# Four fused image layers on one core: layer 0's output statistics by ACT, attention stored compactly, a third exponential tile, and another order in search and q

## The chip, the cores and the metric

The kernel runs on one core of a Trainium2 chip. A core has a matrix engine (TensorE, PE in the tables), a vector engine (VectorE, DVE), a scalar engine for activations (ScalarE, ACT), a general engine (GpSimd, POOL) and an engine that here only issues transfers (SyncE, SP). Each engine executes its own instructions in its own order and waits on semaphores for the others. DMA queues move data between the device's memory and the on-chip memory SBUF; products of PE land in PSUM, which has eight banks of 512 fp32 columns on 128 partitions, and ACT and DVE read them there. The metric is device time in microseconds (us) of one execution; of several executions the median is given.

## The reference

The input is 16 images of 64 x 64 tokens with 256 channels, in fp32. Four layers follow each other, each added to its input, and each working on a group-normalized copy of it (32 groups of 8 channels; mean and variance over the group's channels and all tokens of an image):

```
def _gn(v, G=32, eps=1e-5):                      # (v - mean) / sqrt(var + eps), by image and group

# layer 0: the nearest of 1024 codes, by distance
indices = argmin(sum(x*x) + sum(e*e) - 2 x @ e);   quantized = e.T[indices]
# layer 1: attention within each image row of 64 tokens
attn = sigmoid(einsum('bhik,bhjk->bhij', f, g));   out = einsum('bhij,bhjo->bhio', attn, h)
# layer 2: a gate from a softmax over all 4096 tokens
sim = x0[:, :, None] * x1[:, None, :];   sm = softmax(sim, axis=1)
gate = sigmoid(einsum('bn,bnm->bm', x2, sm));   out = gate * x
# layer 3: linear attention with 4 heads of 32
q = softmax(q, over a head's 32) * SCALE;   k = softmax(k, over tokens)
context = einsum('bhdn,bhen->bhde', k, v);   out = einsum('bhde,bhdn->bhen', context, q)
out = layernorm(out @ w_out + b_out) * gamma + beta
```

f, g and h are projections of the tokens to 32, 32 and 256 channels; x0, x1 and x2 are projections to one number per token; q, k and v to 128 each.

## The kernel before

**Stages.** An image goes through six stages, written as Python generators: `stats0` (statistics of the input), `stage1` (layer 0, called search below), `layer1`, `rows2` and `stage2` (layer 2's rows and exponentials), `gate2` (layer 2's gate, applied), `stage3` (layer 3). Between stages the image lies in device memory, as eight chunks of 512 tokens, transposed: a chunk is a tile of 128 partitions x 2 halves of the channels x 512 tokens. Each stage also gathers the statistics that the next stage's normalization needs.

**What sets the order.** Each generator yields after a piece of work with a number, the piece's share of the stage. A planner at the end of `tile_net_kernel` gives every stage of every image a start and a length in units of one image's search (`task`, with LAG1, LEN1 and the like), and a heap then takes the piece that is due next. So six stages of different images are interleaved. That order is a priority: the tile framework's scheduler sets each engine's order of instructions by it and by what is ready, and `tc.high_priority` lifts a block above the rest. Loads are issued on SP, stores of some results on ACT's queue, gathers on POOL's.

**Buffers.** A pool has rings of buffers, by tag; a tile waits until the ring's oldest is free. PSUM has four single banks (`bank`) for nearly every product and two double ones (`wide`).

**Search** (`stage1`, one image: 8 chunks of 4 token tiles of 128). For each token tile PE computes pd, the products with 1024 codes, in a double bank (L382); ACT writes nn, minus the norms of codes and token (L377); DVE adds both and takes the maximum (L389, a custom instruction), then its index (L394); POOL gathers the code's row onto the tokens (L395). Between the tiles stand a chunk's other steps: `load` of the transposed chunk, `tokens` (load of the tokens), `norm` (ACT normalizes and squares, L327 and L330; PE sums the squares, px, L336; ACT copies them, xrow, L341; PE transposes, pxt, L343), `norm_rows` (DVE copies the norms, L348) and `back`: PE transposes the chunk with its codes back to channels (pt, L357), ACT copies it from PSUM (L360), DVE takes `bn_stats` of it (`chunk_stats`, L254), and ACT's queue stores it (L363). `back(ch - 1)` is called after the third tile of chunk ch, `norm(ch + 1)` after the second. `gn_finish` makes scale, minus mean and their product for the next layer of these statistics, by small products with group matrices.

**Layer 1.** `attend` computes f and g (pfg, L465) and h (ph, L476) of a chunk, and scores of two image rows at a time (psc, L494): 128 x 128 products, of which only the two diagonal blocks of 64 x 64 are used. ACT takes the Tanh of those blocks into one of two attention tiles `attn`, whose other blocks stay zero (L497), and scales them (L500). `mix` multiplies h by the whole 128 x 128 tile (po, L509), and DVE adds the result to the chunk (L513).

**Layer 2's exponentials.** For 32 token tiles and two halves of the tokens, ACT writes the exponentials of 2048 products into a tile ex (L619, with a sum), and DVE multiplies them by x2 and sums (L622). ex has two buffers.

**Layer 3.** For each chunk: k's products and exponentials, q and v (pqv, L751), then the exponentials of q over a head, its sum and normalization (L770 to L776, DVE, POOL and ACT), a product with k's exponentials (pc, L780). `queries(ch - 1)` transposes the normalized q and stores it. After the last chunk come `queries(7)`, and, at high priority, the context product with the output weights and a small Gram matrix. The second loop (`form`, `variance` and the output products po, L849) reads q again.

`put_row` makes a row of 256 values in three bf16 parts, `h_row`, `qv_row` and `x_row`, kept twice side by side; a product with ones adds it to two token tiles.

Of the kernel before, what the change touches and what calls it, by code (L numbers as in the profile page):

```python
# [9 lines left out]
F32 = mybir.dt.float32  # L10
BF16 = mybir.dt.bfloat16
# [5 lines left out]
P = 128  # L17
C = 256
# [23 lines left out]
def kernel(  # L42
# [82 lines left out]
    def row_tile(name):  # L125
        t = const.tile([P, 2, C], BF16, name=name)
        nc.gpsimd.memset(t, 0.0)
        return t

    h_row, qv_row, x_row = row_tile("h_row"), row_tile("qv_row"), row_tile("x_row")  # L130

    def put_row(dst, v, weight, tag, plus=None):
# [11 lines left out]
        nc.scalar.copy(dst[0:PARTS, :, :], row.unsqueeze(1).to_broadcast([PARTS, 2, C]))  # L144
# [43 lines left out]
    w_src = w_qkv.rearrange("(k p) (s n) -> p k s n", p=P, s=3)  # L188


    gam = s3p.tile([P, C], F32, tag="v2", name="gam", bufs=5)
    nc.scalar.dma_start(out=gam, in_=gamma.rearrange("(o n) -> o n", o=1).to_broadcast([P, C]))

    def centred(src, name):
        t = const.tile([P, 2, C], F32, name=name)
        nc.scalar.dma_start(out=t[:, 0, :], in_=src)
        m = small.tile([P, 1], F32, tag="cen", name=f"cen_{name}")
        nc.vector.tensor_reduce(m, t[:, 0, :], AX.X, ALU.add)
        nc.vector.tensor_scalar(m, m, -1.0 / C, None, ALU.mult)
        nc.vector.tensor_scalar(t[:, 0, :], t[:, 0, :], m, None, ALU.add)  # L200
        nc.vector.tensor_tensor(t[:, 1, :], t[:, 0, :], gam, ALU.mult)
        return t

    wo2 = centred(w_out, "wo2")


    bo2 = centred(b_out.rearrange("(o n) -> o n", o=1).to_broadcast([P, C]), "bo2")
    nc.vector.tensor_scalar(bo2, bo2, float(DH ** 0.5 / HEADS), None, ALU.mult)
# [27 lines left out]
    attn = []  # L236
    for n in range(2):
        t = const.tile([P, CH, P], F32, name=f"attn_{n}")
        nc.vector.memset(t, 0.0)
        attn.append(t)  # L240

# [14 lines left out]
    def gn_finish(st, kind, b):  # L256

        tag = f"{kind}_{b}"
        mv = small.tile([P, NK, 2], F32, tag="gn_mv", name=f"mv_{tag}")
        for k in range(NK):  # L260
            nc.vector.bn_aggr(mv[:, k, :], st[:, k, :, :].rearrange("p c s -> p (c s)"))
        mean = mv[:, :, 0]
# [45 lines left out]
    def stage1(b):  # L308
        tag = f"s1_{b}"
        scale, _, nbias = norm0.pop(b)  # L310
# [39 lines left out]
        st1 = stats_tile(1, f"st1_{tag}")  # L350
        x1_d[b] = []

        def back(ch):
            for k in range(NK):
# [5 lines left out]
                nc.scalar.copy(xt[ch][:, k, :], pt)  # L360
            chunk_stats(st1, xt[ch], ch)
# [10 lines left out]
        for ch in range(NCHUNK):  # L372
            for t in range(CH):
# [27 lines left out]
                if t == 1:  # L401
                    if ch + 1 < NCHUNK:
                        norm(ch + 1)
                        yield 2
# [535 lines left out]
```

## Time and profile before

| what | us |
|---|---|
| three runs | 6006.36, 5981.41, 6005.67; median 6005.67 |
| the profiled execution | 5985.76 |
| its span, first to last instruction | 5984.0 |
| largest groups: exponentials with sum on DVE (L622) / on ACT (L619) | 2369.4 / 2138.8 |
| pd on PE (L382) | 2013.5 |
| maximum and index on DVE (L389, L394) | 620.5 and 623.5 |
| nn on ACT (L377) | 585.1 |
| POOL's gathers (L395) | 1084.0 |
| mean granted TensorE clock | 0.949 of full speed |

A row of the profile gives a line, the engine, the operation, the tiles written and read, how often, the busy time and mean duration, and then the idle time of the engine just before such instructions with what ended it. An fp32 product shows as two records on PE, so 2048 products of pd are 4096 records; their ends are modelled, and successive ones overlap. PEld is PE's loading of weights. The reading of an accumulator is an instruction of its own on ACT and DVE.

### The profile page before, as it was taken

How to read it: one execution, taken by the hardware profiler on the slowest of the kernel's cores; microseconds unless marked ns; L12 is line 12 of the kernel's file. 1: busy time of each engine (PE TensorE's matmuls, PEld its weight loads, DVE VectorE, ACT ScalarE, POOL GpSimd, SP SyncE). 2: the span in 40 equal slices, each digit the busy share in tenths (PEclk: the TensorE clock that was granted, in tenths of full speed). 3: DMA queues.
4: the chain of work that ended last, by engine and by line, in shares of the span. 5: the costliest groups of instructions: out<-in, count | busy, mean ns of one | idle time of the engine just before them, and what ended most of it. 6: DMA issues, size and time to landing. Idle time of an engine off the chain costs nothing.

```text
span 5984.0 us, 73947 instructions
## 1 busy us (share of the span) xinstructions
PE 5310.6 (89%) x25167; PEld 3208.0 (54%) x25167; DVE 5132.9 (86%) x7270; ACT 4756.8 (79%) x7138; POOL 1873.7 (31%) x1314
## 2 busy tenths in 40 slices
PE   8978798989989899998989989898999989887777
PEld 3535355545556465554646556464655646464445
DVE  6589698899989899898989989898998989888862
ACT  4578597878888797888979788797988879787763
POOL 3222224233332333323333332433333333312231
PEclk9989899999999999999999999999999999998788
DMA  6453645665656657565665746566475655545543
GB/s 185 143 160 112 209 132 186 187 187 158 207 165 201 194 160 227 149 210 163 197 212 156 224 151 207 172 199 203 153 223 160 204 183 172 188 140 176 170 144 111
DMA packets 521359, 1059.10 MB, mean 177 GB/s; under 512 B 52504, under 2 KB 266392, under 8 KB 512792
## 3 DMA queue, kind: packets, MB, share of 16 engines
q1 hardware_dynamic: 406288, 885.11, 44.6%
q0 software_dynamic: 73728, 67.14, 7.8%
q10 hardware_dynamic: 40968, 102.13, 4.5%
q8 instruction: 200, 3.28, 0.2%
q14 instruction: 175, 1.43, 0.1%
HBM read 751.18 MB, written 303.04 MB: 176 GB/s over the span
## 4 chain that ended last, share of the span: by engine, by line
PE 48%; DVE 21%; ACT 15%; issue 7%; DMA 5%; POOL 4%; ACTq 0%; SPq 0%; POOLq 0%; DVEq 0%
PE pd_s L382 16%; DVE ex_s L622 10%; ACT ex_s L619 6%; PE ph_l L476 4%; PE pqv_s L751 4%; PE po_s L849 3%; DVE i_s L394 2%; PE pk_s L729 2%; PE pr_r L567 2%; DVE nd_s L389 2%; PE po_l L509 2%; POOL xc_s L395 2%; PE pvr_s L829 1%; DVE st_s L254 1%; PE pc_s L780 1%
## 5 line engine op out<-in xcount | busy, mean ns | idle before, releaser
L622 DVE CUSTOM_DVE_ANT_0 ex_s<-ex_s,x2b 128x2048 f32<-128x2048 f32 x1024 | 2369.4, 2318 | 135.9 <-ACT ex_s L619 133.5
L619 ACT ACTIVATE ex_s<-x0b,nmax_s,x_r 128x2048 f32<-128x2048 f32 x1024 | 2138.8, 2089 | 64.7 <-DVE num_s L622 55.0
L382 PE MATMUL pd_s<-e,xn_s 128*128 128x512 f32 x4096 | 2013.5, 621 | 87.6 <-DVE m L389 63.8
L395 POOL DMA_INDIRECT xc_s<-in_emb_rows,i_s x512 | 1084.0, 2117 | 1962.9 <-DVE i_s L394 1460.6
L382 PEld LDWEIGHTS pd_s<-e,xn_s 128*128 128x128 f32 x4096 | 750.6, 196 | 830.4 <-issue 655.0
L389 DVE CUSTOM_DVE_ANT_0 nd_s<-pd_s,nn_s 128x1024 f32<-128x1024 f32 x512 | 620.5, 1212 | 114.8 <-PE pd_s L382 85.4
L394 DVE FIND_INDEX8 i_s<-m,nd_s 128x8 uint32<-128x1024 f32 x512 | 623.5, 1218 | 0.0
L377 ACT ACTIVATE nn_s<-ne,nx_s 128x1024 f32<-128x1024 f32 x512 | 585.1, 1145 | 10.6 <-DVE nx_s L348 3.4
L476 PE MATMUL ph_l<-wh_l,xt_l 128*128 128x256 f32 x2048 | 534.6, 396 | 28.6 <-DVE xt_l L513 20.6
L751 PE MATMUL pqv_s<-wqv_s,xk_s 128*128 128x256 f32 x2048 | 491.9, 381 | 2.9 <-ACT xt_s L360 2.9
L476 PEld LDWEIGHTS ph_l<-wh_l,xt_l 128*128 128x128 f32 x2048 | 381.7, 194 | 155.1 <-issue 61.2
L751 PEld LDWEIGHTS pqv_s<-wqv_s,xk_s 128*128 128x128 f32 x2048 | 388.4, 191 | 130.1 <-issue 63.3
L832 POOL TENSOR_TENSOR lrs_s<-lrs_s,mhalf 128x4 f32<-128x4 f32 x128 | 187.6, 1465 | 651.5 <-ACT lrs_s L831 638.0
L849 PE MATMUL po_s<-wctx_s,qo_s 128*128 128x256 f32 x1024 | 329.4, 412 | 63.5 <-ACT y_s L852 59.8
L852 ACT ACTIVATE y_s<-po_s,lrs_s 128x256 f32<-128x256 f32 x512 | 236.0, 470 | 147.5 <-PE po_s L849 104.3
L327 ACT ACTIVATE xn_s<-xt_s,nb_n,s_n 128x512 f32<-128x512 f32 x256 | 202.4, 806 | 108.2 <-DMA xt_s<-in_xT 98.6
L776 POOL TENSOR_TENSOR qv_s<-qv_s,qd_s 128x512 f32<-128x512 f32 x128 | 167.2, 1307 | 385.3 <-DVE qd_s L775 312.8
L509 PE MATMUL po_l<-attn,h_l 128*128 128x128 f32 x2048 | 280.7, 283 | 7.3 <-DVE m L389 5.2
L509 PEld LDWEIGHTS po_l<-attn,h_l 128*128 128x128 f32 x2048 | 259.9, 195 | 45.8 <-issue 22.1
L849 PEld LDWEIGHTS po_s<-wctx_s,qo_s 128*128 128x128 f32 x1024 | 178.0, 199 | 194.5 <-ACT y_s L852 123.9
L729 PE MATMUL pk_s<-xk_s,wk_s 128*128 128x512 f32 x512 | 256.6, 623 | 0.0
L860 DVE TENSOR_TENSOR y_s<-pxo_s,y_s 128x512 f32<-128x512 f32 x256 | 174.1, 683 | 91.4 <-ACT y_s L852 91.3
(197 smaller groups left out, 7707.6 us busy)
## 6 DMA issues: line engine op xcount, KB each, us to landing
xs_s<-in_xT SPq DMA_DIRECT2D x128, 512.0 KB
xt_s<-in_xT SPq DMA_DIRECT2D x128, 512.0 KB
xc_s<-in_x SPq DMA_DIRECT2D x128, 512.0 KB
x_s<-xt_s ACTq DMA_DIRECT2D x128, 512.0 KB
xt_l<-x_s SPq DMA_DIRECT2D x128, 512.0 KB
x_l<-xt_l SPq DMA_DIRECT2D x128, 512.0 KB
xr_r<-x_l SPq DMA_DIRECT2D x128, 512.0 KB
xg_g<-x_l SPq DMA_DIRECT2D x128, 512.0 KB
```

The source lines that it names most:

```text
L377: nc.scalar.activation(nn, ne2, AF.Identity, bias=nx2[ch][:, t : t + 1])
L382: nc.tensor.matmul(pd[:, cols], lhsT=xn[ch][:, k, t * P : (t + 1) * P], rhs=e2[:, k, cols], start=(k == 0), stop=(k == NK - 1),)
L389: nc.vector.tensor_tensor_reduce(out=nd, in0=pd, in1=nn, scale=1.0, scalar=-3.0e38, op0=ALU.add, op1=ALU.max, accum_out=m8[:, 0:1],)
L394: nc.vector.max_index(i8, m8, nd)
L395: nc.gpsimd.indirect_dma_start(out=xc[ch][:, t, :], out_offset=None, in_=emb_rows, in_offset=bass.IndirectOffsetOnAxis(ap=i8[:, 0:1], axis=0),
L476: nc.tensor.matmul(ph[:, t, :], lhsT=X[:, k, t * P : (t + 1) * P], rhs=wh_n[:, k, :], start=(t % 2 == 0 and k == 0), stop=False, skip_grou ...
L509: nc.tensor.matmul(po[:, k, t * P : (t + 1) * P], lhsT=hs[ch][:, t, k * P : (k + 1) * P], rhs=at[:, t, :], start=True, stop=True,)
L619: nc.scalar.activation(ex, x0b, AF.Exp, bias=nmax[:, T : T + 1], scale=x01[:, T, 1:2], accum_out=den[:, h, T : T + 1])
L622: nc.vector.tensor_tensor_reduce(out=ex, in0=ex, in1=x2b, scale=1.0, scalar=0.0, op0=ALU.mult, op1=ALU.add, accum_out=num[:, h, T : T + 1],)
L729: nc.tensor.matmul(pk, lhsT=wk_n[:, k, :], rhs=xt[:, k, :], start=(k == 0), stop=(k == NK - 1))
L751: nc.tensor.matmul(pqv[:, j, :], lhsT=xt[:, k, t * P : (t + 1) * P], rhs=wqv_n[:, k, :], start=(j == 0 and k == 0), stop=False, skip_group ...
L849: nc.tensor.matmul(po[:, j, :], lhsT=qT[:, t * P : (t + 1) * P], rhs=wctx[:, 1, :], start=True, stop=True)
```

## The change

- **Statistics of layer 0's output.** In `back`, ACT's copy from PSUM also gives the sum over the tokens, and a second activation squares the same bank in place, shifted by layer 0's mean, and gives the sum of squares. `chunk_stats` is no longer called there. At the end of `stage1` five small DVE operations make mean and variance from the sums, and `gn_ends`, the second half of `gn_finish`, goes on from them.
- **Compact attention.** The attention tile holds only the 64 x 64 blocks: two image rows on the two halves of the partitions. Scores are products of 64 x 64; ACT's Tanh and scaling work on 128 partitions at once; `mix` makes two products with 64 rows each where there was one with 128, into two banks, and DVE's addition reads them in the chunk's order. The two zeroed `attn` tiles are gone.
- **Room.** The rows `h_row`, `qv_row`, `x_row` are kept once and read twice (`twice`); w_out and b_out are kept without their copy scaled by gamma, which is multiplied in once per image; two small tiles share buffers with others (wT with wk_n, gram with ctx_bd); the ring v2 has four buffers instead of five. ex has three buffers instead of two.
- **Order in search.** `back(ch - 1)` is called after the second tile of a chunk, `norm(ch + 1)` after the third, `norm_rows` after the fourth.
- **Order in q.** The sum, reciprocal and multiplication that normalize q become `normalize`, called for a chunk when the next one begins; `queries` of the last chunk is called after the high-priority block.
- **Planner.** Layer 1 of image 0 gets a length of 0.2 instead of 0.35. In `stage2` the gate's yields are split in two.

```diff
         def back(ch):
...
-                nc.scalar.copy(xt[ch][:, k, :], pt)
-            chunk_stats(st1, xt[ch], ch)
+                nc.scalar.activation(xt[ch][:, k, :], pt, AF.Copy, accum_out=st1[:, 0, k, ch : ch + 1])
+                nc.scalar.activation(
+                    pt, pt, AF.Square, bias=nshift[:, k : k + 1], accum_out=st1[:, 1, k, ch : ch + 1]
+                )
...
-                if t == 1:
-                    if ch + 1 < NCHUNK:
-                        norm(ch + 1)
-                        yield 2
-                if t == 2:
+                if t == 1 and ch > 0:
+                    back(ch - 1)
+                    yield 2
+                if t == 2 and ch + 1 < NCHUNK:
+                    norm(ch + 1)
+                    yield 2
+                if t == 3:
                     if ch + 1 < NCHUNK:
                         norm_rows(ch + 1)
-                    if ch > 0:
-                        back(ch - 1)
-                        yield 2
-                if t == 3:
-                    if ch + 1 < NCHUNK:
                         tokens(ch + 1)
                     if ch + 2 < NCHUNK:
                         load(ch + 2)
         back(NCHUNK - 1)
         with tc.high_priority(offset=URGENT):
-            norm1[b] = gn_finish(st1, "n1", b)
+            nc.vector.tensor_reduce(sums, st1, AX.X, ALU.add)
+            nc.vector.tensor_scalar(mv[:, :, 0], sums[:, 0, :], 1.0 / TOK, None, ALU.mult)
+            nc.vector.tensor_tensor(off, mv[:, :, 0], nshift, ALU.add)
+            nc.vector.tensor_tensor(off, off, off, ALU.mult)
+            nc.vector.scalar_tensor_tensor(
+                mv[:, :, 1], sums[:, 1, :], 1.0 / TOK, off, op0=ALU.mult, op1=ALU.subtract
+            )
+            norm1[b] = gn_ends(mv, "n1", b)
...
-            at = attn[ch % 2]
+            at = ats[ch] = s1p.tile([P, CH, ROW], F32, tag="at", name=f"at_{tag}_{ch}")
+            psc = [bank(f"psc_{tag}_{ch}_{n}").rearrange("p (t i) -> p t i", i=ROW) for n in range(2)]
+            for t in range(2):
+                for r in range(2):
+                    cols = slice(t * P + r * ROW, t * P + (r + 1) * ROW)
+                    for n in range(2):
+                        part = slice(n * CK, (n + 1) * CK)
+                        nc.tensor.matmul(
+                            psc[n][r * ROW : (r + 1) * ROW, t, :], lhsT=fg[part, 1, cols], rhs=fg[part, 0, cols],
+                            start=True, stop=True,
+                        )
             for n in range(2):
...
+                nc.scalar.activation(at[:, 2 * n : 2 * n + 2, :], psc[n][:, 0:2, :], AF.Tanh, scale=0.5)
+            nc.scalar.activation(at, at, AF.Identity, scale=0.5, bias=half)
...
         def mix(ch):
+            at, h = ats.pop(ch), hs.pop(ch)
+            po = wide(f"po_{tag}_{ch}").rearrange("p (r m i) -> p r m i", r=2, i=ROW)
+            for k in range(NK):
+                for t in range(CH):
+                    for r in range(2):
+                        rows = slice(r * ROW, (r + 1) * ROW)
+                        nc.tensor.matmul(
+                            po[:, r, k * CH + t, :], lhsT=h[rows, t, k * P : (k + 1) * P], rhs=at[rows, t, :],
+                            start=True, stop=True,
+                        )
+            X = xt[ch].rearrange("p k n -> p (k n)").rearrange("p (m r i) -> p m r i", r=2, i=ROW)
+            nc.vector.tensor_tensor(X, po.rearrange("p r m i -> p m r i"), X, ALU.add)
...
-                    ex = s2p.tile([P, TOK // 2], F32, tag="ex", name=f"ex_{tag}_{h}_{T}", bufs=2)
+                    ex = s2p.tile([P, TOK // 2], F32, tag="ex", name=f"ex_{tag}_{h}_{T}", bufs=3)
...
+        def normalize(ch):
+            q4 = qvs[ch][:, :, 0, :].rearrange("p t (h d) -> p t h d", d=DH)
+            qd = small.tile([P, CH, HEADS], F32, tag="qd", name=f"qd_{tag}_{ch}")
+            nc.vector.tensor_reduce(qd, q4, AX.X, ALU.add)
+            nc.vector.reciprocal(qd, qd)
+            nc.gpsimd.tensor_tensor(q4, q4, qd.unsqueeze(3).to_broadcast([P, CH, HEADS, DH]), ALU.mult)
...
             nc.sync.dma_start(out=xt, in_=x3[ch])
+            if ch > 0:
+                normalize(ch - 1)
...
-        queries(NCHUNK - 1)
+        normalize(NCHUNK - 1)
         rk = small.tile([P, 1], F32, tag="rk", name=f"rk_{tag}")
...
         yield 4
+        queries(NCHUNK - 1)
...
-        end = task("layer1", b + 1 + LAG1, LEN1 if left and b else 0.35, layer1(b), 88)
+        end = task("layer1", b + 1 + LAG1, (LEN1 if b else 0.2) if left else 0.35, layer1(b), 88)
```

## The prediction

> **What bounds the kernel now.** I read the busy time of the engines first, then the same by stretch of the run, then the chain that ended last.
>
> ```profile
> PE 5310.6 (89%) x25167; PEld 3208.0 (54%) x25167; DVE 5132.9 (86%) x7270; ACT 4756.8 (79%) x7138; POOL 1873.7 (31%) x1314
> ...
> PE 48%; DVE 21%; ACT 15%; issue 7%; DMA 5%; POOL 4%; ACTq 0%; SPq 0%; POOLq 0%; DVEq 0%
> ```
>
> ```profile
> 900.00:5200.00 4300.00, 3947.58 (x19020) 2390.83 (x19018) 3880.94 (x5465) 3601.90 (x5396) 1432.54 (x978) 0.97 0.60 186
> 5200.00:5984.00 784.00, 600.87 (x2778) 410.42 (x2777) 548.37 (x775) 538.08 (x879) 195.46 (x172) 0.86 0.44 148
> ```
>
> The columns of the second fence are the stretch, its length, then PE, weight loads, DVE, ACT and POOL. Between 900 and 5200 us five or six stages of different images run together: PE is busy 92% (3948 of 4300), DVE 90%, ACT 84%. No engine is full; each waits now and then for another, and the chain passes through all three. So a microsecond is worth less than a microsecond. My exchange rate is an engine's time on the chain over its busy time: PE 0.48 x 5984 / 5311 = 0.54, DVE 0.21 x 5984 / 5133 = 0.24, ACT 0.15 x 5984 / 4757 = 0.19. All terms below are first counted on their engine, then multiplied by this. It is a first-order rate: it fails where an engine becomes full.
>
> **Statistics by ACT.** DVE loses 256 passes (L254 of st_s<-xt_s) and, of gn_finish, 32 aggregations of 0.34; it gains five tiny operations per image, at 0.17 to 0.24 each (the rows of L600 to L606) 1 us, 16 in all. 164 + 11 - 16 = 159 us off DVE. Gone with them is a wait, 54.6 us in which DVE, a strict queue, stood before ACT's copy with everything behind it.
>
> ```profile
> L254 DVE BATCH_NORM_STATS2 st_s<-xt_s 128x6 f32<-128x512 f32 x256 | 163.8, 679 | 54.7 <-ACT xt_s L360 54.6
> ...
> L360 ACT COPY xt_s<-pt_s 128x512 f32<-128x512 f32 x256 | 138.5, 584 | 50.3 <-PE pt_s L357 49.6
> ...
> L738 ACT ACTIVATE kx_s<-pk_s,nkm_s 128x512 f32<-128x512 f32 x128 | 86.4, 675 | 4.5 <-DVE nkm_s L732 4.4
> ...
> L719 ACT ACTIVATE qT_s<-pq_s 128x512 f32<-128x512 f32 x128 | 77.0, 601 | 29.1 <-PE pq_s L717 28.9
> ...
> L738 ACT ACTIVATION_READ_ACCUMULATOR kx_s<-pk_s,nkm_s 128x1 f32 x128 | 25.0, 196 | 0.0
> ```
>
> ACT's copy becomes an activation with a sum: 601 (L719, same shape out of PSUM) + 196 (the read of the accumulator, a row of its own) against 584, so +213 ns. The Square is new: 675 (L738, a bias per partition, out of PSUM) + 196 = 871. No row writes to PSUM; the bounds are the plain copy's 576 (L756) and the Square from SBUF, 804 (L330), each + 196. 256 x 1.084 = 277 us (252 to 310). In weights: -39 (DVE) +53 (48 to 59, ACT) -13 (wait) = +1. Behind the Squares on ACT's queue stands the store of the layer's output (L363); it leaves 2.1 us later, but back() is called one token tile earlier, about 11 us (a period of 351 us, read below, over 32 tiles).
>
> The Trainium skill speaks against this part: "ScalarE: Activation LUTs", Rules for kernel authors, puts multiplications and other plain arithmetic on VectorE, up to about three times faster per element in bf16. Here, in fp32, the rows are 871 against 679; by the rule alone the part would lose 277 - 159 = 118 us of engine time and should not be done. The rows of the busy time say that DVE is the fuller engine, which the rule does not look at.
>
> **Compact attention.** Per chunk ACT had four Tanh (L497, 270) and two Identity (L500, 506), 2.09 us; it keeps two and one on full partitions with the same elements in a row, 1.05. 128 x 1.04 = 133 us off ACT, -25. On PE each score product shrinks to 64 columns and weights of 64, and mix makes two half-height products (64 rows, 64 columns) where one full one was. What matters is whether products on different rows of the array run together. L494 shows it:
>
> ```profile
> 1507.44 0.71 PE L494 MATMUL psc_l<-fg_l 32*128 32x128 f32 x4
> 1508.07 0.94 PE L509 MATMUL po_l<-attn,h_l 128*128 128x128 f32 x6
> 1508.94 0.71 PE L494 MATMUL psc_l<-fg_l 32*128 32x128 f32 x4
> ...
> ```
>
> ```profile
> 1542.61 0.53 PEld L494 LDWEIGHTS psc_l<-fg_l 32*128 32x128 f32 x8
> 1542.61 0.72 PE L494 MATMUL psc_l<-fg_l 32*128 32x128 f32 x8
> ```
>
> Four records of one row group take 0.71 us, and eight of two groups, loads included, 0.72. So I let mix's halves run together: 16 steps of 128-column weights each, as before, 0. Bounds: halves one after the other add 16 steps of about 0.11 us (0.72 us less the last record's 0.27, over four steps), 1.8 us x 128 = +230; if a step fell to half with its columns, -115. The scores' steps halve, about 0.3 us x 128 = -40 (0 to -60). But a change of tile shape empties the array:
>
> ```profile
> 1997.90 1.83 PE pr_r L567 x4
> 1999.73 3.63 PE pd_s L382 x8
> 2003.36 0.44 PE prt_r L576 x4
> 2003.80 3.44 PE pd_s L382 x8
> ```
>
> Eight records of pd take 3.63 us after weights of 32 columns (pr_r) and 3.44 after the same shape: 0.19. In the order of the built programs PE changes shape 1433 times before and 1739 after: 306 x 0.19 = +58. PE net +18, weight +10. Part: -15 (-75 to +110).
>
> **Third exponential tile.** It is for these two waits, the first DVE's, the second ACT's; the weights of all of it are -33 and -10:
>
> ```profile
> DVE ex_s L622 <- ACT ex_s L619: 133.5, 118, 3.9
> ...
> DVE qd_s L774 <- ACT qv_s L772: 70.6, 57, 3.0
> ...
> ACT ex_s L619 <- DVE num_s L622: 55.0, 49, 4.7
> ```
>
> The exponential pair is even (DVE 2318 + 82, ACT 2089 + 190 ns a tile), so a buffer helps against jitter, not against a slower partner: half, -21 (-43 to 0).
>
> **Order in search.** back() one token tile earlier frees the input buffer sooner, hence the load two chunks on; ACT waits 98.6 us for those loads (L327, 37.5 of them between 900 and 5200). Half, -9 (-19 to 0). The normalization one tile later, with four activations, sixteen records and a transpose on PE and a copy on DVE, shortens the cover of the next chunk's first nn; SP's loads stay at the fourth tile. By ACT's own rows, ACT has a median of 18.5 us of work between xrow and that nn before and 12.8 after, but 2.3 in the tightest tenth. DVE now waits 33.9 us there (L348); doubling it is +8 (0 to +25).
>
> **Order in q.** The normalization of q (DVE 0.68 and 0.24, POOL 1.3) moves to the next chunk's start, past POOL's gathers and running sums; POOL is 31% busy. DVE's 70.6 us before ACT's exponential go (-17). queries() of the last chunk (four transposes, a copy, a store on ACT's queue) moves behind the urgent context product; it is read eight chunks later. PE stood 51.7 us for POOL there (L717) and 49.5 at a normalization's first product behind DVE's qd (L264). At 0.54 these are -28 and -27. What is late next is the context product, which needs the same last chunk, so I take half of all: -36 (-72 to 0). The v2 ring of four instead of five costs nothing: in program order the buffer that ek takes was read a chunk earlier; without that cover the price is one 0.6 us copy a chunk, 128 x 0.6 x 0.19 = 15.
>
> **Smaller.** Layer 1 of image 0 is compressed from 0.35 to 0.2 of a period, so its exponentials start up to 53 us earlier, while DVE is little used: -5 (-20 to 0). Narrower rows, half-width w_out product: 48 copies 0.2 shorter and 32 records 0.2 shorter: -6. PSUM: ACT now holds the two banks of a back() for 3.3 us instead of 1.2. In the built order 43 of 256 such banks have less than 3.3 us of PE work before their next writer: 43 x 1 us x 0.54, about +20 (0 to +80).
>
> **Sum.** +1 -15 -21 -9 +8 -36 -5 -6 +20 = -63 us against a span of 5984.0, so 5921; 2 us lie around the span (5985.8), and the median of the runs, 6005.67, stands 20 above this execution: 5943. I say 5945, its own range 5900 to 5985.
>
> **Rivals.**
> Mix's halves do not overlap: for it, L494 has 32 rows and no 64-row product is in the trace; against it, the fence above. +124 on my sum, 6065, slower; it decides as soon as half of the steps are serial. Chance 0.09.
> ACT takes DVE's place: the four activations in a row hold banks, and PE stands. Place: the writer after pt. Price: 2.1 us x 128 pairs x 0.54 = +145 if all held, 6090; from two pairs in five (+58) it eats the gain. For it, four banks serve everything small; against it, the 213 banks with room. Chance 0.13.
> PE is the bound, and what DVE is spared becomes waiting for PE: then only PE's own +18 and its two waits count, near 6000, no change. For it, PE at 92%; against it, PE's idle time, which by the list of waits is about 240 us for DVE and 270 for ACT. Chance 0.20.
> DVE was the true limit: its weights count in full, waits too (-39 -13 -33 -17 -55 beyond ACT's +28): about -130, 5875. Chance 0.12.
>
> **How the numbers follow.** The forecast keeps 0.46. A measurement tells about 0.5% from no change, 30 us. Faster than that: 0.46 + 0.12 = 0.58; within it 0.20; slower 0.09 + 0.13 = 0.22. The range for 8 in 10 reaches from 5860 (the full weights) to 6055 (half of either slow rival).
>
> **What would show it.** DVE near 4975 us busy, ACT near 4890, PE 5330; the Square near 0.68 and its accumulator reads near 0.2; no DVE wait for the copy; mix's sixteen steps near 0.11 with both halves interleaved; DVE's and ACT's waits at the exponentials about halved; the period between images, now 351 us (the first pd of image 6 at 1703 us, the last pd of image 15 at 5209), near 347. A mix that takes 3.6 us a chunk, or PE waiting for the Square by more than 100 us, would make the prediction wrong.

## The result, and the profile after

No change: 5996.07 us after (median of 20 runs), 5992.35 us before (20 runs on the same chip), ratio 1.0004, 95% interval 0.9993 to 1.0015. The forecast was 5945 us: 61 us below the median of the three runs known before (6005.67), 47 below the median of these twenty. The first fence is the page of the changed kernel, with its engines' busy times and the chain that ended last; the second is the same stretch of the run as was shown of before.

```profile
PE 5346.5 (90%) x28239; PEld 3210.7 (54%) x28239; DVE 5007.1 (84%) x7074; ACT 4752.2 (80%) x7522; POOL 1971.2 (33%) x1314
...
PE 53%; DVE 15%; ACT 13%; DMA 5%; issue 5%; POOL 3%; ACTq 0%; SPq 0%; POOLq 0%; DVEq 0%
```

```profile
900.00:5200.00 4300.00, 3978.85 (x21372) 2398.66 (x21371) 3781.00 (x5304) 3598.72 (x5685) 1517.86 (x971) 0.95 0.59 185
```

DVE was spared 126 us (159 were forecast), PE has 36 us more, ACT has what it had. (PE's busy time is not only its work: b_dve0 below has the products of the kernel before, one for one, and shows 5341.7.) The period between images (mean over images 3 to 15, by the first pd of each) went from 346.9 to 350.2 us; the tail after the last pd, from 775 to 711 us. What a faster end won, the steady part lost. These are two single executions, and the one after (5971.22 us) is the fastest of its twenty; it took 14.5 us less than the one before.

ACT's groups of the change (line, operation, busy time in us, mean ns of one):

```profile
L360 ACT ACTIVATE pt_s<-pt_s,nm_n 128x512 f32<-128x512 f32 x256 | 169.7, 663 | 0.0
L359 ACT ACTIVATE xt_s<-pt_s 128x512 f32<-128x512 f32 x256 | 153.2, 598 | 47.1 <-PE pt_s L356 46.4 <-issue 0.7
...
L360 ACT ACTIVATION_READ_ACCUMULATOR pt_s<-pt_s,nm_n 128x1 f32 x256 | 54.6, 213 | 0.0
L359 ACT ACTIVATION_READ_ACCUMULATOR xt_s<-pt_s 128x1 f32 x256 | 53.2, 208 | 0.0
```

The durations are those forecast, but they do not add up. In the timeline of ACT (start in us, length) each read starts before its activation ends, and the next activation starts inside the read:

```profile
2337.80 0.59 ACT L359 ACTIVATE xt_s<-pt_s 128x512 f32<-128x512 f32 x1
2338.28 0.20 ACT L359 ACTIVATION_READ_ACCUMULATOR xt_s<-pt_s 128x1 f32 x1
2338.37 0.66 ACT L360 ACTIVATE pt_s<-pt_s,nm_n 128x512 f32<-128x512 f32 x1
2338.94 0.21 ACT L360 ACTIVATION_READ_ACCUMULATOR pt_s<-pt_s,nm_n 128x1 f32 x1
2339.03 0.60 ACT L359 ACTIVATE xt_s<-pt_s 128x512 f32<-128x512 f32 x1
```

A copy with its square takes 1.23 us (2339.03 - 2337.80), where the durations sum to 1.66. So ACT's time for this part, overlaps counted once, rose from 131 to 322 us, by 191 and not 277. Attention's, counted the same way, fell from 261 to 101. PE's groups of the compact attention:

```profile
L522 PE MATMUL po_l<-at_l,h_l 64*128 64x64 f32 x4096 | 299.3, 286 | 25.0 <-DVE xt_l L527 21.7 <-ACT at_l L510 1.8 <-DVE m L390 1.4
...
L504 PE MATMUL psc_l<-fg_l 32*64 32x64 f32 x2048 | 86.8, 241 | 1.8 <-ACT qv_s L780 1.3
```

Mix's halves run together: the records start in pairs, 6 to 13 ns apart, then 105 ns to the next pair. Of the lists of waits (engine, what waits, for what; us in all, times, longest), these are of the changed kernel:

```profile
DVE nd_s L390 <- ACT nn_s L378: 106.9, 70, 7.3
DVE ex_s L636 <- ACT ex_s L633: 105.6, 75, 4.8
...
ACT ex_s L633 <- DVE num_s L636: 12.1, 16, 2.4
...
PEld pkt_s L786 <- ACT pt_s L360: 6.3, 11, 0.6
```

and this of the kernel before:

```profile
DVE nd_s L389 <- ACT nn_s L377: 14.2, 18, 3.2
```

DVE no longer waits for layer 0's copy (54.6 before). The two waits at the exponentials, which were to be halved, went from 133.5 to 105.6 us (DVE) and from 55.0 to 12.1 (ACT). But DVE waits 106.9 us for nn, 14.2 before. PE hardly waits for the Square: 6.3 us is the largest entry, of weight loads. Against the forecast's marks: DVE 5007 us (4975 forecast), ACT 4752 (4890), PE 5346 (5330), the Square and mix's steps as forecast, the period longer instead of shorter. The new wait for nn, 93 us of DVE, would be some 22 us at the prediction's weight, less than half of the gain that is missing.

### The profile page after: what moved, and what is told of

Read it like the earlier page. It is cut to its first block, busy times and chain, and to the rows that moved or that the text cites. A ratio compares the mean times of both kernels' runs of the same rounds, so it can differ in the third digit from the quotient of the medians.

```text
span 5969.5 us, 80122 instructions
## 1 busy us (share of the span) xinstructions
PE 5346.5 (90%) x28239; PEld 3210.7 (54%) x28239; DVE 5007.1 (84%) x7074; ACT 4752.2 (80%) x7522; POOL 1971.2 (33%) x1314
## 4 chain that ended last, share of the span: by engine, by line
PE 53%; DVE 15%; ACT 13%; DMA 5%; issue 5%; POOL 3%; ACTq 0%; SPq 0%; POOLq 0%; DVEq 0%
PE pd_s L383 18%; DVE ex_s L636 6%; ACT ex_s L633 5%; PE ph_l L484 4%; PE po_s L870 4%; PE pqv_s L775 3%; PE po_l L522 3%; PE pk_s L753 3%; PE pr_r L581 2%; PE pz_s L842 2%; DVE i_s L395 2%; POOL qv_s L795 2%; ACT nn_s L378 2%; PE pvr_s L850 2%; PE pxo_s L875 2%
## 5 line engine op out<-in xcount | busy, mean ns | idle before, releaser
L636 DVE CUSTOM_DVE_ANT_0 ex_s<-ex_s,x2b 128x2048 f32<-128x2048 f32 x1024 | 2380.6, 2330 | 106.6 <-ACT ex_s L633 105.6
L633 ACT ACTIVATE ex_s<-x0b,nmax_s,x_r 128x2048 f32<-128x2048 f32 x1024 | 2138.5, 2089 | 21.0 <-DVE num_s L636 12.1
L383 PE MATMUL pd_s<-e,xn_s 128*128 128x512 f32 x4096 | 2074.5, 635 | 70.8 <-DVE m L390 37.0
L390 DVE CUSTOM_DVE_ANT_0 nd_s<-pd_s,nn_s 128x1024 f32<-128x1024 f32 x512 | 622.4, 1216 | 230.1 <-ACT nn_s L378 106.9
L484 PE MATMUL ph_l<-wh_l,xt_l 128*128 128x256 f32 x2048 | 521.1, 388 | 31.4 <-DVE xt_l L527 26.4
L853 POOL TENSOR_TENSOR lrs_s<-lrs_s,mhalf 128x4 f32<-128x4 f32 x128 | 170.9, 1335 | 800.6 <-ACT lrs_s L852 746.0
L522 PE MATMUL po_l<-at_l,h_l 64*128 64x64 f32 x4096 | 299.3, 286 | 25.0 <-DVE xt_l L527 21.7
L522 PEld LDWEIGHTS po_l<-at_l,h_l 64*128 64x128 f32 x4096 | 267.3, 196 | 92.5 <-issue 29.5
L795 POOL TENSOR_TENSOR qv_s<-qv_s,qm_s 128x512 f32<-128x512 f32 x128 | 212.6, 1661 | 269.4 <-DVE qm_s L794 148.2
L744 POOL TENSOR_TENSOR qv_s<-qv_s,qd_s 128x512 f32<-128x512 f32 x128 | 181.4, 1418 | 240.0 <-DVE qd_s L743 147.6
```

Source lines behind the costliest of these rows:

```text
L383: nc.tensor.matmul(pd[:, cols], lhsT=xn[ch][:, k, t * P : (t + 1) * P], rhs=e2[:, k, cols], start=(k == 0), stop=(k == NK - 1),)
L390: nc.vector.tensor_tensor_reduce(out=nd, in0=pd, in1=nn, scale=1.0, scalar=-3.0e38, op0=ALU.add, op1=ALU.max, accum_out=m8[:, 0:1],)
L484: nc.tensor.matmul(ph[:, t, :], lhsT=X[:, k, t * P : (t + 1) * P], rhs=wh_n[:, k, :], start=(t % 2 == 0 and k == 0), stop=False, skip_grou ...
L522: nc.tensor.matmul(po[:, r, k * CH + t, :], lhsT=h[rows, t, k * P : (k + 1) * P], rhs=at[rows, t, :], start=True, stop=True,)
L633: nc.scalar.activation(ex, x0b, AF.Exp, bias=nmax[:, T : T + 1], scale=x01[:, T, 1:2], accum_out=den[:, h, T : T + 1])
L636: nc.vector.tensor_tensor_reduce(out=ex, in0=ex, in1=x2b, scale=1.0, scalar=0.0, op0=ALU.mult, op1=ALU.add, accum_out=num[:, h, T : T + 1],)
```

## The experiments

Every kernel was run beside the kernel before on the same chip; differences in us are the ratio less one, times its time there (5992 to 6001). Where a run is told with a theory: W is the prediction with its weights, the others are named as they came up.

**The parts alone.** C was the theory that PE's half-clock stretches behind mix's small products eat the gain, P that PE is the bound.

b_att has only the compact attention put into the kernel before, b_stat only the statistics by ACT. Of each edit some lines are shown, ahead of what was expected. b_att:

```diff
...
-                    nc.scalar.activation(at[rows, 2 * n : 2 * n + 2, rows], psc[rows, 0:2, rows], AF.Tanh, scale=0.5)
...
+                nc.scalar.activation(at[:, 2 * n : 2 * n + 2, :], psc[n][:, 0:2, :], AF.Tanh, scale=0.5)
...
```

> The kernel before with the compact attention alone (scores of 64 x 64, mix in two halves of 64 rows). Theory C (clock): the trace after has 447 us at half the TensorE clock between 900 and 5200 us, 266 before, and 177 us of it begin right behind windows full of mix, none before; so mix's halves pull the clock down, and PE loses about half of 177 us. C expects here the half-clock time of that stretch near 440 us and a time 35 to 70 us above before. Theory P (PE is full): only PE's own busy time counts, +36 us in the trace after; P expects +20 to +40 us and nothing of the clock. Theory W (the weights of the prediction, PE 0.54, DVE 0.24, ACT 0.19): +19 for PE, -30 for ACT, so -11 us.

b_stat:

```diff
...
-                nc.scalar.copy(xt[ch][:, k, :], pt)
-            chunk_stats(st1, xt[ch], ch)
+                nc.scalar.activation(xt[ch][:, k, :], pt, AF.Copy, accum_out=st1[:, 0, k, ch : ch + 1])
+                nc.scalar.activation(
+                    pt, pt, AF.Square, bias=nshift[:, k : k + 1], accum_out=st1[:, 1, k, ch : ch + 1]
+                )
...
```

> The kernel before with the statistics of layer 0's output by ACT alone. DVE loses about 160 us and its 55 us of waits for the copy, ACT gains about 190 (the accumulator reads overlap in the trace after). W expects -39 - 13 + 36 = -16 us; C the same, since PE's work is untouched; P expects 0 within 10 us. A rival, that ACT holds the PSUM banks too long, expects +30 us or more and new waits of PE for ACT's Square.

a_ex2 is the changed kernel with two exponential tiles (`bufs=2`), a_ex2_full that one with attention as before. a_ex2, then a_ex2_full:

> The kernel after with two exponential tiles instead of three; it is the base for the next run too. W expects +21 us against after; P expects 0 within 10 us.

> The kernel after with two exponential tiles and the attention as it was before (zeroed 128 x 128 tiles, mix over 128 rows). Against the run with two exponential tiles alone: C expects the half-clock time between 900 and 5200 us back near 270 us, none of it behind mix, and 35 to 70 us less time although ACT gets 160 us more to do; P expects 20 to 40 us less, by PE's busy time, and the clock unchanged; W expects +11 us.

Measured: b_att 0.9928 (0.991 to 0.9946), -43; b_stat 1.0116 (1.0095 to 1.0136), +70; a_ex2 1.0047 (1.0029 to 1.0064), so the third tile is worth some -26; a_ex2_full 1.0124 (1.0104 to 1.0144), so attention is worth -46 there. C falls: attention gains. P falls as well. The parts add up to the result with nothing left for the new orders in search and q. In b_stat DVE waits more for ACT's exponentials (133.5 before):

```profile
DVE ex_s L637 <- ACT ex_s L634: 224.7, 192, 5.6
```

From this I formed theory A: ACT's time is the dear one (0.36 to 0.4 per us), DVE's is worth nothing.

**Theory A put to the test.** a_nostat is the changed kernel with bn_stats back on DVE. b_dve0 spares DVE and no other engine: it leaves out the statistics of seven of eight chunks. b_pe is to spare PE alone: it leaves the row x_row out of the output. b_stat_sb asks whether the square holds the PSUM bank too long (theory R).

a_nostat:

> The changed kernel with the statistics of layer 0's output back on DVE (bn_stats of the SBUF copy, as before); compact attention, three exponential tiles and the changed orders stay. DVE's busy time rises by about 130 us, ACT's occupied time falls by about 190 us. Theory A (ACT's time is what the change pays for, DVE's relief is worth about nothing): the part cost 69 us when it was done alone, so taking it out of the changed kernel gives that back: 5925 to 5945, a ratio to the kernel before of 0.988 to 0.992. Theory W (the weights of the prediction): DVE +126 x 0.24 = +30, a wait for the copy +11, ACT's busy time falls by 12 or so: about +40 or no less than +20, so 6015 to 6040, 1.003 to 1.007. If the two parts only cost each other (the statistics are dear only where ACT is full of attention's halves): within 10 us of the changed kernel, 0.998 to 1.002.

b_dve0:

```diff
...
-            chunk_stats(st1, xt[ch], ch)
+            if ch == 0:
+                chunk_stats(st1, xt[ch], ch)
...
```

> The kernel before with bn_stats of layer 0's output for the first of 8 chunks only; it leaves out the statistics of the other seven, and nothing is put on ACT in their place. DVE loses about 7/8 of 173 us, 150 us, and most of its waits for the copy (55 us). It measures what DVE's relief alone is worth. Theory W: 0.24 x 150 + 11 = -47, so about 5950, ratio 0.992. Theory A: -10 to 0, ratio 0.998 to 1.000, because DVE's time there lies beside ACT's and PE's. If DVE were the limit: -100 or more, 0.983 or less.

b_stat_sb, against b_stat:

```diff
...
-                    pt, pt, AF.Square, bias=nshift[:, k : k + 1], accum_out=st1[:, 1, k, ch : ch + 1]
+                    junk, xt[ch][:, k, :], AF.Square, bias=nshift[:, k : k + 1], accum_out=st1[:, 1, k, ch : ch + 1]
...
```

> The kernel before with statistics by ACT, but the square read from the SBUF copy and written to a bf16 scratch tile, so that the PSUM bank comes free after the first activation, as before (the constant rows are kept once, to make room, as in the changed kernel). It tells the bank's longer hold from ACT's longer time. Theory R (the bank held for the second activation is what costs): the 69 us of that part alone come back for the most part, ratio 0.998 to 1.003. Theory A (ACT's time is the cost): about as dear as with the square in PSUM, ratio 1.009 to 1.014.

b_pe:

```diff
-                nc.tensor.matmul(px, lhsT=ones3, rhs=x_row, start=False, stop=True, skip_group_check=True)
```

> The kernel before without the product that adds x_row in layer 3's output loop (it leaves that row out of the output): PE loses about 57 us of busy time, no other engine changes. It measures what PE's time alone is worth. Theory W: 0.54 x 57 = -31, ratio 0.995. If PE is the bound outright: -57, ratio 0.9905. Theory A (ACT dear, PE at most as in W): between 0 and -31, ratio 0.995 to 1.000.

Measured: a_nostat 0.9884 (0.9859 to 0.9909), -70; b_dve0 1.0017 (1.0004 to 1.0029), +10; b_stat_sb 1.0106 (1.0087 to 1.0125), +64; b_pe 1.0027 (1.0014 to 1.004), +16. A held on a_nostat and b_stat_sb and was the nearest on the other two; R fell. But one would not expect a kernel that only has work taken out to become slower, and two did. (b_pe is a poor test of PE: its PE is busy 5301.9 us, 8.7 less than before where 57 were expected, at a median granted clock of 0.9375 against 0.946 for the runs of the kernel before beside it.) So the next runs put ACT's time to the test by itself, and work the other way.

b_actplus:

> The kernel before with one more ACT instruction behind each copy of layer 0's output into SBUF: a copy of a constant (128x512) to a bf16 scratch tile that nobody reads (the constant rows are kept once, to make room). ACT gets 256 instructions of about 0.58 us, some 150 us, and nothing else waits for them or is relieved. It measures ACT's time by itself. Theory A (time added to ACT anywhere in the loop is dear, 0.36 to 0.4 per us): +54 to +60, ratio 1.009 to 1.010. Theory W (0.19): +28, ratio 1.005. If statistics by ACT were dear for their own chain (the accumulators, the sums that layer 1 waits for) and not for ACT's time: +10 or less, ratio 1.000 to 1.002.

```diff
...
                 nc.scalar.copy(xt[ch][:, k, :], pt)
+                nc.scalar.copy(junk, ne2[:, 0:CW])
...
```

a_nostat_cp, its edit against a_nostat:

> The changed kernel with layer 0's output statistics back on DVE, and the copies of that output from PSUM moved from ACT to DVE as well: ACT loses 256 copies of 0.59 us, 150 us, DVE gets as many of 0.55 to 0.68 us, 140 to 175 us. It asks whether moving work the other way than the change did helps further. Theory A: -0.36 x 150 = -54 for ACT, and DVE's time for nothing up to half price (0 to +40, because DVE would stand at 88% of the span): 5885 to 5930, ratio 0.981 to 0.988. Theory W: -0.19 x 150 + 0.24 x 157 = +9 on that kernel's 5940, ratio 0.990 or more. If both engines sit on one chain, each as dear as the other: as that kernel, 0.988 to 0.990.

```diff
-                nc.scalar.copy(xt[ch][:, k, :], pt)
+                nc.vector.tensor_copy(xt[ch][:, k, :], pt)
```

a_nostat_os, then a_nostat_oq:

> The changed kernel with layer 0's output statistics back on DVE, and the order in search as it was before (norm of the next chunk at tile 1, its rows and back at tile 2). The prediction had the new order in search at -1 (-9 for a wait, +8 for another): by it, and by theory A, the same as with the new order, ratio 0.987 to 0.990. If the new order is a loss that the other gains pay for: 20 or more below that, 0.985 or less. If it is the gain: 0.992 or more.

> The changed kernel with layer 0's output statistics back on DVE, and the order in q as it was before (sums and quotients straight after the exponential, the last queries ahead of the context). The prediction had the new order at -36 (-72 to 0): ratio 0.994 (0.988 to 1.000). The sum of the runs so far leaves nothing for it: 0.986 to 0.990.

Measured: b_actplus 0.9957 (0.9943 to 0.9971), -26: faster, although by its page ACT is busy 134 us more than before:

```profile
PE 5302.8 (89%) x25167; PEld 3210.3 (54%) x25167; DVE 5131.1 (86%) x7270; ACT 4890.4 (82%) x7394; POOL 1913.6 (32%) x1314
```

a_nostat_cp 1.0126 (1.0102 to 1.0149), 145 us slower than a_nostat; a_nostat_os 1.0036 (1.0021 to 1.0051), 91 slower; a_nostat_oq 0.9885 (0.9862 to 0.9908), the same. A does not fit: added ACT time gained, and ACT's relief at DVE's cost lost.

**What all these edits share.** The source's order is a priority only. The build's scheduler sets each engine's order by it and by what it reckons to be ready, so any added or removed instruction moves others, all through the program. In the built programs I counted the instructions that stand behind another number of pd products (on PE), of nn (ACT) or of indices (DVE) than in the kernel compared with: b_actplus 865 of 15,579 on PE, 140 of 6,386 on ACT, 160 of 6,758 on DVE; b_dve0 2,347 on PE; b_stat 2,479; the changed kernel against a_nostat 2,217 of 17,115. They move by little: of b_actplus' 865 on PE 96% by half a token tile or less, none by more than one.

So the last runs hold the order. Behind the last traced instruction stands

```diff
+        for a, b in zip(line, line[1:]):
+            tc.add_manual_dep(b, a.name, info, reason="order")
```

where `line` is one engine's instructions in the order read from another kernel's build, and the edge is one of order only, with no wait. An instruction that the other kernel lacks stands behind its predecessor in the source. Theory O: what moved the time was the order. The runs, in turn: p_actplus, p_ordact, p_stat, p_att, p_after, p_dve0.

> The kernel before with the 256 idle ACT copies, but every engine's instructions held in the order that they have in the kernel before (each extra copy stands right behind the copy of layer 0's output that it follows in the source). So it shows the price of 150 us of ACT time by itself. Theory A: +54 (ratio 1.009). Theory W: +28 (1.005). Theory O (the build orders the instructions anew for every edit, and that new order, not the added time, is what moved the time by -24): a cost between the two bounds of no cost and full cost, which the next run has to balance: this one's difference and the next one's sum up to about -24.

> The work of the kernel before, instruction for instruction, in the order that the build gave to the kernel with the 256 idle copies (those left out). Nothing but the order differs from the kernel before. Theory O: clearly off 1.000, by -24 less the price of ACT's time: 0.985 to 0.996. If order is worth nothing: 0.998 to 1.002, and the idle copies themselves would have made the kernel faster.

> The kernel before with statistics by ACT (the run that came out at +69), every engine's other instructions held in the order of the kernel before; each square stands right behind its copy, the five small DVE steps stand where the two aggregations stood. Theory A: the same +69 (1.010 to 1.013), as it is ACT's time that is paid. Theory O: much of the +69 was the order: between -10 and +40 (0.998 to 1.007). Theory W: -13 for DVE's wait, -39 for DVE, +53 for ACT's activations, which really took +191 us of its time in place of 277, so +36: about -16 (0.997).

> The kernel before with compact attention (the run that came out at -43), every engine's other instructions held in the order of the kernel before; two of the half-height products stand where one product stood. Theory A: the same -43 (0.991 to 0.995). Theory O: some of it was the order: 0.992 to 1.002. Theory W as predicted: -15 (0.9975).

> The changed kernel, all its work, but every engine's instructions held in the order that the build gave to the changed kernel without its statistics by ACT (the one that came out at 0.988); each square stands right behind its copy, the five small DVE steps where the two aggregations stood. The changed kernel as built came out at 1.000. Theory O (statistics by ACT cost some 19 us by themselves, as with the order of the kernel before, and the rest of the 60 us between the two kernels is the order that the build chose): 0.990 to 0.994, so 35 to 60 us faster than the changed kernel as built. If the part itself costs the 60 us: 0.998 to 1.002.

> The kernel before with bn_stats of layer 0's output for the first of 8 chunks only (it leaves out the statistics of the other seven), every engine's other instructions held in the order of the kernel before. With its own order it came out at +10 us. It shows what relief of DVE by 133 us, with the wait for the copy, is worth by itself. Theory W (the weight 0.24, and -11 for the wait): -43, ratio 0.993. By the run of statistics by ACT with the order held (+19, of which ACT's 191 us at the 0.2 of the idle copies are +38): -19, ratio 0.997. If DVE's time is worth nothing: 0.999 to 1.001.

Measured, with the run of the same work in the order that its own build chose beside it:

| work | own order | order held | the order's share |
|---|---|---|---|
| kernel before, in b_actplus' order (p_ordact) | | 0.9928 (0.9915 to 0.9942) | -43 |
| idle ACT copies (b_actplus, p_actplus) | 0.9957, -26 | 1.0049 (1.0036 to 1.0063), +29 | -55 |
| DVE spared (b_dve0, p_dve0) | 1.0017, +10 | 0.9927 (0.9912 to 0.9943), -44 | +54 |
| statistics by ACT (b_stat, p_stat) | 1.0116, +70 | 1.0032 (1.0018 to 1.0046), +19 | +50 |
| compact attention (b_att, p_att) | 0.9928, -43 | 0.9888 (0.9866 to 0.9909), -67 | +24 |
| the whole change, in a_nostat's order (after, p_after) | 1.0004, +2 | 0.9899 (0.9882 to 0.9916), -61 | +63 |

In every row the same work in another order takes another time, by 24 to 63 us, and the intervals do not overlap. The first row has not one instruction of other work: there the order alone is shown to move the time. (It and the second row look at the same two orders.) O's forecasts of the sizes held for p_actplus, p_ordact and p_stat, and p_after came out at their edge; p_att missed: O had expected that some of its -43 was a gift of the order (0.992 to 1.002), and its own order had cost it 24 instead. For p_dve0 the weights (-43) were right and the -19 reckoned from p_stat was not. The verdicts on the earlier theories were read from builds in their own orders; with the order held C and P fall again (-67 in p_att, -44 in p_dve0) and A does too (+29 where it had +54, +19 where it had +69), but R was not run again. And the whole change, all of it, is 61 us faster than the kernel before in an order that the build chose for a kernel with one part less. But the kernel before gains from a new order too: between p_ordact and p_after lie only 0.0029, some 17 us, so what the change is worth depends on the orders that are compared. (With the order come the buffers that a ring gives to each tile; the runs do not part the two. Nor do they part it from the clock: in five of the six pairs the faster order had the higher granted clock, in the median of its runs by 0.003 to 0.009 - 0.941 in p_after, 0.932 in the changed kernel - and in p_att and b_att it was the same. Whether the clock carries some of the order's effect or follows from the shorter waits stays open.)

The two prices are read where the order is held. p_actplus has the idle copies in its groups, 0.63 us each:

```profile
L365 ACT CAST junk<-ne 128x512 bf16<-128x512 f32 x256 | 160.6, 627 | 0.4
```

29 us for 160.6 us of ACT: 0.18 per us. p_dve0 against b_dve0 shows what the order does to the same work. First the pages' busy times, p_dve0 and then b_dve0:

```profile
PE 5296.5 (89%) x24866; PEld 3210.0 (54%) x25167; DVE 4999.7 (84%) x7046; ACT 4754.5 (80%) x7138; POOL 1870.2 (31%) x1314
```

```profile
PE 5341.7 (89%) x25167; PEld 3213.1 (53%) x25167; DVE 4999.9 (83%) x7046; ACT 4752.4 (79%) x7138; POOL 1916.5 (32%) x1314
```

DVE and ACT do the same to a quarter of a us and 2 us (PE's record is short by 301 matmuls in the first, so its busy times cannot be compared). The spans are 5962.5 and 6010.6. The waits, again p_dve0 and then b_dve0:

```profile
DVE ex_s L623 <- ACT ex_s L620: 183.0, 144, 3.9
...
ACT xn_s L327 <- DMA xt_s<-in_xT: 99.0, 35, 7.5
```

```profile
DVE ex_s L623 <- ACT ex_s L620: 223.4, 174, 3.9
ACT xn_s L327 <- DMA xt_s<-in_xT: 149.1, 35, 7.7
```

40 us at the exponentials, 50 at a load, others elsewhere on PE and POOL: the difference is spread over waits that the edit did not touch. Which displaced instruction starts it was not found, and for p_ordact it cannot be read from the trace: its profiled execution took 5988 us, the six others 5956 to 5965.

## Why the prediction was wrong

The forecast of -60 us was wrong, and its rival at 6000 had the time right by luck, for a wrong reason. That p_after came out at -61 is luck as well, for its parts are not those of the sum. Point by point:

**The step that failed** is the sum: "All terms below are first counted on their engine, then multiplied by this", and added up as though the rest of the program kept its place. It looked at the built order for two counts only, tile shapes and PSUM banks. There was no term for the order that the build gives anew to everything else, neither in the sum nor in the range. That term is 24 to 63 us either way in six pairs, as large as the whole forecast; in the changed kernel it was about +63 against a_nostat's order, and against that order it took the gain. The changed kernel in the order of the kernel before was not run. Beside it two terms of the sum were mis-sized: compact attention (-15 for -67 with the order held) and the order in q (-36, and taking it out changed nothing).

**The weights** held in the two held runs that move one engine's time alone. ACT 0.19: measured 0.18. DVE 0.24, and -13 for the wait: by them p_dve0's 133 us and the wait make -45, measured -44. They did not give the price of attention (below).

**Statistics by ACT**, +1 and with the bank's hold +20: ACT's time was mis-sized (by p_stat's page +184 us of busy time in place of 277, since the reads overlap), and DVE lost 138 in place of 159. With those sizes the terms are -33 - 13 + 35 + 20 = +9; measured +19 (11 to 28) with the order held, and +9 in a_nostat's order (0.9899 against 0.9884, with intervals of 0.0017 and 0.0025). Whether the bank's 20 belongs there was not shown: b_stat_sb ran in its own order. For it speaks that in p_stat the entries of PE's waits for the Square add up to 20 us and those of its weight loads to 55, where before those for the copy made 8 and 20. The Trainium skill's rule that the prediction named against this part ("ScalarE: Activation LUTs", Rules for kernel authors) came out on the right side, at 19 us of time and not at the 118 us of engine time that the prediction had reckoned by it: the part should not be done here, and the changed kernel without it is at 0.9884.

**Compact attention**, -15: mix's halves ran together as forecast; ACT's relief was 160 us for 133 (-30 for -25). The +18 for PE came out at +2: with the order held PE's busy time is 5312.6 us against 5310.6. Its groups, before and then p_att:

```profile
L382 PE MATMUL pd_s<-e,xn_s 128*128 128x512 f32 x4096 | 2013.5, 621 | 87.6 <-DVE m L389 63.8 <-ACT xn_s L327 15.0 <-DVE xt_l L513 4.6
...
L509 PE MATMUL po_l<-attn,h_l 128*128 128x128 f32 x2048 | 280.7, 283 | 7.3 <-DVE m L389 5.2 <-ACT h_l L485 1.5 <-ACT attn L500 0.6
...
L494 PE MATMUL psc_l<-fg_l 32*128 32x128 f32 x1024 | 117.0, 297 | 0.2 <-DVE ctx_s L782 0.2
```

```profile
L376 PE MATMUL pd_s<-e,xn_s 128*128 128x512 f32 x4096 | 2039.6, 628 | 71.6 <-DVE m L383 53.5 <-ACT xn_s L321 14.3 <-DVE xt_l L511 2.3
...
L506 PE MATMUL po_l<-at_l,h_l 64*128 64x64 f32 x4096 | 287.0, 283 | 6.5 <-DVE m L383 4.7 <-ACT h_l L479 1.7
...
L489 PE MATMUL psc_l<-fg_l 32*64 32x64 f32 x2048 | 72.4, 233 | 27.2 <-ACT xt_s L354 21.9 <-ACT fg_l L466 2.2 <-ACT y_s L850 1.7
```

The scores fell by 45 us (40 were forecast), mix took 6 more and pd 26 more. The 0.19 us for a change of tile shape came from one pair of rows; over the whole trace of before, the median of eight pd records without a wait is 3.70 us behind another shape (32 cases) and 3.60 behind the same (148), so 0.10, and the 306 changes would be 31 us and not 58. How much of pd's 26 they are, and how much is the lower clock (0.943 in this execution, 0.949 before), is not shown. The terms with these sizes make about -29; -67 was measured, so some 38 us have no term. Some of them may stand in PE's waits for ACT in layer 3, before and p_att:

```profile
PEld po_s L849 <- ACT y_s L852: 123.9, 143, 5.4
...
PE po_s L849 <- ACT y_s L852: 59.8, 66, 5.0
```

```profile
PEld po_s L847 <- ACT y_s L850: 76.8, 114, 5.3
...
PE po_s L847 <- ACT y_s L850: 34.0, 39, 5.0
```

A reading that no run tests: an ACT queue that is shorter by 160 us serves others sooner, and the weight from the chain does not count that.

**Third tile**, -21: measured -26 (a_ex2), both in their own orders, so the closeness proves little. **Order in q**, -36: nothing (a_nostat_oq), also in its own order. **Order in search**, -1: the old order cost 91 us (a_nostat_os), of which the part that the moved steps themselves have is not known: that run was in its own order.

**The rivals.** "PE is the bound, and what DVE is spared becomes waiting for PE" is refuted by p_dve0, where DVE's relief pays 44 us. Were DVE the limit, that relief should have brought -100 or more, as was expected of b_dve0. Mix did not run serially, and the largest entry of waits for the Square on PE and its weight loads is 6.3 us; what the banks' hold costs is open, as said.

**What stays open:** what PE's time is worth with the order held (b_pe became slower in its own order, at a lower clock), why DVE's copies cost a_nostat_cp 145 us, more than any order's share seen here, which places in the order matter, what part the clock has in it, and where the rest of attention's gain comes from.

## What to carry to other kernels

Where a scheduler in the build sets the order, an edit has two effects, its own price and a new order for the rest; an experiment that edits a part measures both, so hold the order (edges of order between an engine's instructions) before a price is read from it. Here two prices came out as reckoned once the order was held, attention's did not, and the order's share was up to 1% either way: that belongs in the range of any forecast, and it can be had as a gain, for the same work in another order was 43 us faster for the kernel before and some 60 for the changed one. A theory that comes nearest in four runs (ACT is dear) can still be wrong; and so can the run that takes it down: b_actplus was faster by its new order alone, and only with the order held did it show what ACT's time costs.

## What the hardware showed

An activation's sum cost ACT some 0.09 us, less than the 0.2 us of its read, which overlaps both neighbours: a copy with its sum starts the next activation 0.57 us after its own start (median of 249 pairs, after), and a plain copy that the next copy follows directly 0.48 us (109 pairs, before). In the stretch from 900 to 5200 us the granted clock of PE fell from 0.97 to 0.95, in stretches at half clock of 3.4 to 10 us before and up to 20 us after: 266 us of them before, 447 after. In 22 of those after (177 us) mix's products of 64 rows and 64 columns took the largest part of PE's time in the 3.4 us ahead of the stretch; before, mix did so in 2 (7 us). Yet the profiled execution of p_after has 464 us at half clock there and is 14 us shorter (span 5955.5 against 5969.5), and p_att, which has the same products and 0.96 there, is among the fastest. So these stretches alone do not decide the time.
